# Attention: the halves of the weight sums are added directly behind the next chunk's key product

## The chip, the cores and the metric

The kernel runs on one core of one Trainium2 chip. The metric is the device time of one execution in microseconds (us); lower is better. Three runs of the kernel before took 2790.14, 2790.73 and 2792.69 us, so the time before is the median, 2790.73 us. The profiled execution is a further run with a time of its own, 2798.62 us, and all durations below are from it.

Engine names as the profile writes them: PE is TensorE's matmul, PEld its weight load, DVE is VectorE, ACT is ScalarE, POOL is GpSimd, SP is SyncE. `L708` is line 708 of the kernel before.

## The reference

Four layers over 2048 nodes, a batch of 8 and 128 features, all with the same sparse adjacency matrix (about 1 in 128 entries set). Layers 0 and 1 are masked attention with 8 heads of 16 features, then a projection, a layer norm, a feed-forward net and a second layer norm. Layers 2 and 3 are graph attention (GAT); the change does not touch them.

```python
# layers 0 and 1
Q, K, V = h @ Wq, h @ Wk, h @ Wv            # as (B, N, 8 heads, 16)
scores = einsum('bnhd,bmhd->bhnm', Q, K) / sqrt(16)
scores = where(adj_matrix == 0, -inf, scores)
attn = softmax(scores, axis=-1)
attn_out = einsum('bhnm,bmhd->bnhd', attn, V)
x = layer_norm(h + attn_out @ Wo + bo)
x = layer_norm(x + relu(x @ W1 + b1) @ W2 + b2)
# layers 2 and 3
h = x @ W
e = leaky_relu((h @ a_src)[:, :, None] + (h @ a_dst)[:, None, :])
out = softmax(where(adj == 0, -inf, e)) @ h
x = layer_norm(out + x)
```

The softmax's denominator, the sum of a node's weights per batch entry and head, is what the changed lines compute.

## The kernel before, in words

**Tiling.** The adjacency is turned into lists of neighbours, and nodes are sorted by how many they have. A block is 128 nodes, one per partition; there are 16 blocks in each layer. A block has as many slots as its longest list (`CAPS`, from 29 in the first block down to 10 in the last). A chunk is two slots in layers 0 and 1: each slot is an indirect DMA that gathers one neighbour's keys and values for all 8 batch entries (1 MB per slot) into one of 7 buffers `kv`. So a block is 5 to 15 chunks, and an attention layer is 141 chunks.

**One chunk** (`attention_chunk`, a generator that `go` advances step by step):

1. key product on DVE: keys times queries (`L657`);
2. on DVE the two halves of each head's products are added (`L663`); PE transposes the result eight times into `pair`, which sums the rest (`turn_into`, `L335`); ACT takes the exponent into `ring` (`L679`);
3. PE transposes the weights back (`L683`), ACT copies them to `weights` (`L687`). In a block's last chunk `block_sums` follows: PE adds up the weights of up to seven chunks (`L636`, `L641`) and ACT copies the sum to the tile `partial` (`L646`), whose left and right 64 columns are the two slots of a chunk;
4. on DVE the values are multiplied by the weights (`L695`);
5. and 6. for each slot PE adds eight transposed tiles to the block's accumulator `acc` (`L335`).

**The order around the change.** Every engine works through its own instructions in the order in which the program issues them, and that order is written out by hand in `layers`. Its loop has one iteration per chunk `c`. Within iteration i the order is: step 3 of chunk i-1; step 6 of chunk i-3; step 1 of chunk i; a `slot`; step 2 of chunk i; a `slot`; then `weigh` for chunk i-2, which is its steps 4 and 5; a `slot`. A `slot` advances each side thread (`threads`, `tails`) by one step and issues gathers (`fetch`).

**The sums.** If the chunk that `weigh` takes is the last of its block (call it X), `weigh` first calls `sums`: on DVE the two halves of `partial` are added into `block_sum` (`L708`), ACT takes the logarithm (`L710`), and a thread `scales` is started, which over the next slots takes an exponent on ACT (`L730`, 128x1024), transposes the result on PE (eight times, `L335` into `m`) and copies it on ACT (`L741`, twice). For the last block of a layer `sums` also reduces the smallest and the largest sum on DVE (`L714`, `L715`). So the sum of block X stands in iteration X+2, behind the key products of X+1 and X+2 and both their `L663`, and ahead of X's own `L695`.

**What uses it.** `tail` is started in iteration X+3, and in the fifth slot after that `outputs` multiplies `acc` by `scale` on DVE (`L723`, twice). Then `attention_tail` runs in the slots, in two halves: projection, both norms, the feed-forward net and the next layer's projection. This is work of PE and ACT (`L754` to `L804`, `normed` at `L502` to `L509`, `project` at `L539` to `L549`), issued between the steps of the next block's chunks.

Of the kernel before, what the change touches and what calls it, by code (L numbers as in the profile page):

```python
# [89 lines left out]
def sparse_path(ctx: ExitStack, tc: tile.TileContext, ins: dict, out: bass.AP, flag: bass.AP):  # L90
# [384 lines left out]
    def reciprocal_sums(l, t, w, columns, folded):  # L475

        sums = small.tile([P, columns], F32, tag="sums", name="sums")
        n = CAPS[t] if t > 0 else BASE
        nc.vector.tensor_reduce(
            sums, w[:, :n, :].rearrange("p s c -> p c s"), axis=AX.X, op=ALU.add  # L480
        )
        if t == 0:
            nc.vector.tensor_add(sums, sums, folded)
        nc.vector.tensor_reduce(dmin[:, l, t : t + 1], sums, axis=AX.X, op=ALU.min)
        nc.vector.tensor_reduce(dmax[:, l, t : t + 1], sums, axis=AX.X, op=ALU.max)
        nc.vector.reciprocal(sums, sums)
        return sums
# [217 lines left out]
    def sums(l, t, box):  # L705
        if l < 2:
            both = box["partial"]
            nc.vector.tensor_add(block_sum[:, t, :], both[:, : NB * NH], both[:, NB * NH :])  # L708
            box["r"] = small.tile([P, NB * NH], F32, tag="logs", name="logs", bufs=1)
            nc.scalar.activation(box["r"], block_sum[:, t, :], AF.Ln)  # L710
            threads.append(scales(l, box))
            if t == NT - 1:
                every = block_sum.rearrange("p t c -> p (t c)")
                nc.vector.tensor_reduce(dmin[:, l, :1], every, axis=AX.X, op=ALU.min)  # L714
                nc.vector.tensor_reduce(dmax[:, l, :1], every, axis=AX.X, op=ALU.max)  # L715
            return
        box["r"] = reciprocal_sums(l, t, box["w"], NB, box.get("folded"))
# [7 lines left out]
    def scales(l, box):  # L725

        box["scale"] = scale = work.tile([P, NB, P], F32, tag="oT", name="scale", bufs=1)
        if l < 2:
            r = box["r"].rearrange("p (b h) -> p b h", h=NH)
            nc.scalar.activation(  # L730
                scale.rearrange("p b (j h) -> p b j h", h=NH),
                r[:, :, None, :].to_broadcast([P, NB, HD, NH]), AF.Exp, scale=-1.0,
            )
            yield
        for i in range(0, NB, 4):
            pt = misc()
            for j in range(4):
                r = box["r"][:, i + j : i + j + 1].to_broadcast([P, P])
                turn_into(pt[:, j * P : (j + 1) * P], scale[:, i + j, :] if l < 2 else r, j == 0)
            yield  # L740
            nc.scalar.copy(scale[:, i : i + 4, :].rearrange("p b n -> p (b n)"), pt)  # L741
# [439 lines left out]
    def advance(group):  # L1181
        for g in list(group):
            if next(g, 0) == 0:
                group.remove(g)

    def fetch():

        while now[1] < len(every):
            c = every[now[1]]
            l, t, k, ns = c["l"], c["t"], c["k"], c["ns"]  # L1190

            if now[1] - now[0] > (5 if now[1] >= KVB and every[now[1] - KVB]["l"] > 1 else 4):
                return
            resorted = l > 0 and t < 2 and not c["folded"]
            need = NT - max([b for end, b in EARLY[t] if k + ns <= end] + [0] if resorted else [0])
            if put[l] < need:
                return
            c["buf"] = buffer()[:, : ns * width(l)].rearrange("p (s c) -> p s c", s=ns)
            c["turn"] = turn[0]
            for i in range(ns):  # L1200
                at = t * BASE if resorted else first[t]
                index = (sorted_lists if resorted else lists)[:, at + k + i : at + k + i + 1]
                gather(l, index, c["buf"][:, i], need)
            now[1] += 1

    def hurry():

        c = every[min(now[0], len(every) - 1)]
        return c["l"] == 2 and c["t"] == NT - 1 or c["l"] > 1 and put[c["l"]] < NT

    def slot():
        advance(threads)
        advance(tails)
        fetch()
        beat[0] += 1
        c = every[min(now[0], len(every) - 1)]
        if c["l"] > 0 and put[c["l"]] < NT or beat[0] % 3 == 0 and hurry():
            advance(tails)

    def drain():  # L1220
        while threads or tails:
            advance(threads)
            advance(tails)

    def later(n, make):
        for _ in range(n):
            yield
        yield from make()

    def tail(l, t, box):  # L1230
        for _ in range(4 if l < 2 else 3 if t > NT - 4 else 5):
            yield
        outputs(l, t, box)
        if l < 2:
            tails.append(later(1, lambda: attention_tail(l, t, box, 0)))
            tails.append(later(4, lambda: attention_tail(l, t, box, 4)))
        else:
            tails.append(later(1, lambda: gat_tail(l, t, box)))
        yield
# [9 lines left out]
    def begin(c):  # L1249
        if c["l"] < 2:  # L1250
            threads.append(attention_begin(c["l"], c["t"], c["box"]))

    def chunk(i):
        return every[i] if 0 <= i < len(every) else dict(l=None, k=None, last=False, folded=False)

    def go(c, times=1):

        for _ in range(times if c["l"] is not None else 0):
            next(c["run"], None)

    def weigh(some, added):

        for c2 in some:
            if c2["last"]:
                sums(c2["l"], c2["t"], c2["box"])
            go(c2, 2)
            added.append(c2)

    def layers():
        drain()  # L1270
        begin(every[0])
        drain()
        for _ in weights:
            pass
        threads.append(find_lists(1))
        weighed, added = [], []
        for i in range(len(every) + 2):
            c1, c, n1, n2 = (chunk(i + j) for j in range(-1, 3))
            for c2 in weighed[-1:]:
                go(c2)  # L1280
            while added:
                c2 = added.pop(0)
                go(c2)
                if c2["last"]:
                    threads.append(tail(c2["l"], c2["t"], c2["box"]))
            now[0] = i
            fetch()
            if c["k"] == 0:
                l, t = c["l"], c["t"]
                if l == 0:  # L1290
                    if t + 2 < NT:
                        threads.append(find_lists(t + 2))
                    if t == 0:
                        threads.append(first_states(range(1, NT)))
                        threads.append(later(12, clear_late))
                    if t in (2, 6):
                        threads.append(order_lists(t // 4))
                while l < 2 and "asked" not in c["box"]:
                    slot()
            while i < len(every) and now[1] <= i:  # L1300
                slot()
            if n2["k"] == 0:
                begin(n2)

            if n1["l"] in (2, 3) and n1["folded"]:
                go(n1)
            if c["l"] not in (0, 1) and weighed:
                weigh(weighed, added)  # L1310
                weighed = []
            if c1["l"] in (2, 3) and c1["last"]:
                sums(c1["l"], c1["t"], c1["box"])
                threads.append(scales(c1["l"], c1["box"]))
            go(c)
            slot()
            go(c)
            slot()
            if c["l"] in (0, 1):
                weighed.append(c)  # L1320
            if len(weighed) > 2:
                weigh(weighed[:1], added)
                weighed.pop(0)
            if c1["l"] in (2, 3):
                go(c1, 2)
                if c1["last"]:
                    threads.append(tail(c1["l"], c1["t"], c1["box"]))
            slot()
        verdict()
        drain()  # L1330

    weights = prepare()
    with tc.manual_schedule():
        nc.scalar.add_instruction(
            mybir.InstLoadActFuncSet(name=nc.get_next_instruction_name(), act_func_set_id=LN_EXP)
        )
        start()
        layers()
# [522 lines left out]
```

## Time and profile before

| | |
|---|---|
| median of three runs | 2790.73 us (2790.14 to 2792.69) |
| profiled execution, its time | 2798.62 us |
| its span (first to last instruction) | 2796.7 us |
| start-up, before the first chunk | about 0 to 150 us |
| layer 0 chunks | about 150 to 1041 us |
| layer 1 chunks | about 1041 to 1887 us |
| layers 2 and 3 | about 1887 to 2797 us |
| sums (`L708`) | 32 in all, 16 per attention layer, 0.23 us each |
| key products (`L657`) | 280, 2.2 us each |
| half additions (`L663`) | 282, 1.2 us each |
| value products (`L695`) | 282, 2.2 us each |

The times of the layers are from the timeline; counts and durations are from the page's costliest groups and from the instructions of the tile `block_sum`. The busy share of an engine is over the whole span. A gap of an engine is put down to what ended last before it. A PE row's duration is modelled and pipelined: eight transposes take about 1.04 us as a row, but the next row starts 0.87 us after it.

### The profile page before, as it was taken

To read this page: it belongs to the slowest core of one execution; us is meant where nothing else is said; L and a number is where in the kernel's file an instruction comes from. 1 tells how busy PE (TensorE), PEld (TensorE's weight loads), DVE (VectorE), ACT (ScalarE), POOL (GpSimd) and SP (SyncE) were. 2 spreads that over 40 slices of the span, in tenths; PEclk is the share of its full clock that TensorE was granted. 3 is DMA by queue.
4 is the path that set the end of the run, shared out by engine and by line. 5 is a ranking of instruction groups with operands and counts; after the bars stand their busy time and mean duration, and the time that the engine had idled before them with its cause. 6 is when DMAs were issued, how large, how long until landed. Compare 5 with 4: busy or idle time off the path is not lost.

```text
span 2796.7 us, 48901 instructions
## 1 busy us (share of the span) xinstructions
PE 2345.7 (84%) x17811; PEld 2126.5 (76%) x17811; DVE 2513.7 (90%) x2467; ACT 1381.6 (49%) x5032; POOL 1755.3 (63%) x1346
## 2 busy tenths in 40 slices
PE   5866889898899998798989999997677887878885
PEld 4655788787788887688878888886567776878885
DVE  9698999999899897999999999986889997799995
ACT  3611444454455665154445556566346566355554
POOL 3367788678656454545565566562776776677772
PEclk9978999999999999999999999999789888999997
DMA  9898999999999888789999999984999998999994
GB/s 365 275 373 311 369 349 345 376 338 350 369 337 355 336 320 315 306 320 369 348 390 369 354 374 368 349 328 172 367 412 413 375 367 326 347 411 413 406 402 157
DMA packets 195426, 973.64 MB, mean 348 GB/s; under 512 B 30012, under 2 KB 31804, under 8 KB 123184
## 3 DMA queue, kind: packets, MB, share of 16 engines
q0 software_dynamic: 172080, 885.06, 82.5%
q1 hardware_dynamic: 18346, 60.00, 5.5%
q10 hardware_dynamic: 4752, 25.36, 2.7%
q8 instruction: 144, 2.36, 0.3%
q14 instruction: 104, 0.85, 0.1%
HBM read 917.09 MB, written 87.36 MB: 359 GB/s over the span
## 4 chain that ended last, share of the span: by engine, by line
PE 42%; DVE 24%; DMA 16%; issue 8%; ACT 8%; POOL 1%; ACTq 0%; POOLq 0%; DVEq 0%; SPq 0%
PE acc L335 15%; DMA kv<-table,lists 9%; DVE kv L695 8%; DVE kv L657 8%; PE pair L335 4%; PE m L793 4%; PE m L776 3%; PE m L539 3%; PE m L342 2%; DVE kv L838 2%; PE m L788 2%; PE m L593 2%; PE m L759 2%; PE m L763 2%; DMA table<-rows,perm 2%
## 5 line engine op out<-in xcount | busy, mean ns | idle before, releaser
L321 POOL DMA_INDIRECT kv<-table,lists x938 | 1282.2, 1367 | 678.0 <-PE acc L335 269.8
L335 PE MATMUL acc<-ident,kv 128*128 128x128 f32 x8048 | 1052.9, 285 | 159.6 <-DVE kv L695 87.9
L335 PEld LDWEIGHTS acc<-ident,kv 128*128 128x128 f32 x8048 | 957.6, 148 | 222.4 <-DVE kv L695 111.1
L695 DVE TENSOR_TENSOR kv<-kv,weights 128x2048 f32<-128x2048 f32 (+1 forms) x282 | 625.8, 2219 | 25.9 <-ACT weights L687 25.8
L657 DVE TENSOR_TENSOR kv<-kv,q 128x2048 f32<-128x2048 f32 (+1 forms) x280 | 618.2, 2208 | 32.0 <-DMA kv<-table,lists 26.3
L838 DVE TENSOR_TENSOR kv<-kv,pair 128x3584 f32<-128x3584 f32 (+1 forms) x150 | 530.8, 3538 | 1.0
L335 PE MATMUL pair<-ident,kv 128*128 128x128 f32 (+1 forms) x2256 | 301.3, 277 | 86.1 <-issue 72.8
L663 DVE TENSOR_TENSOR kv<-kv 128x1024 f32<-128x1024 f32 (+1 forms) x282 | 334.8, 1187 | 9.2
L335 PEld LDWEIGHTS pair<-ident,kv 128*128 128x128 f32 (+1 forms) x2256 | 257.0, 141 | 106.4 <-issue 85.1
L321 POOL DMA_INDIRECT kv<-table,sorted_lists x150 | 192.8, 1286 | 139.7 <-PE acc L335 42.9
L679 ACT ACTIVATE ring<-pair 128x128 f32<-128x128 f32 (+1 forms) x282 | 77.8, 276 | 365.0 <-PE pair L335 292.9
L502 ACT ACTIVATE n<-m,eps 128x128 f32<-128x128 f32 x512 | 181.5, 371 | 137.6 <-PE m L793 133.3
L687 ACT COPY weights<-pair 128x128 f32<-128x128 f32 (+1 forms) x282 | 73.3, 260 | 350.9 <-PE pair L683 342.7
L843 ACT ACTIVATE kv<-kv,ws 128x128 f32<-128x128 f32 x544 | 174.5, 398 | 145.0 <-DVE ws L832 136.4
L793 PE MATMUL m<-w_L,hT 128*128 128x128 f32 x1024 | 157.3, 276 | 0.0
L509 ACT ACTIVATE n<-m,rs 128x128 f32<-128x128 f32 x512 | 146.4, 376 | 0.3
L793 PEld LDWEIGHTS m<-w_L,hT 128*128 128x128 f32 x1024 | 136.1, 193 | 0.0
L776 PE MATMUL m<-n1T,w_L 128*128 128x512 f32 x256 | 132.9, 604 | 3.0 <-ACT hT L781 1.8
L723 DVE TENSOR_TENSOR o<-acc,scale 128x512 f32<-128x512 f32 x128 | 83.3, 684 | 52.0 <-ACT scale L741 27.1
L526 POOL DMA_INDIRECT table<-rows,perm x57 | 82.1, 1441 | 70.1 <-ACT own L562 18.7
L342 PE MATMUL m<-ident,n 128*128 128x128 f32 x640 | 114.9, 293 | 11.9 <-ACT n L509 5.6
L342 PEld LDWEIGHTS m<-ident,n 128*128 128x128 f32 x640 | 79.6, 145 | 51.0 <-ACT n L509 23.3
(254 smaller groups left out, 3614.2 us busy)
## 6 DMA issues: line engine op xcount, KB each, us to landing
kept<-xT SPq DMA_DIRECT2D x40, 512.0 KB, 6.7
kv<-in_adj_dram SPq DMA_DIRECT2D x16, 1024.0 KB, 15.6
table<-kv ACTq DMA_DIRECT2D x16, 1024.0 KB, 4.5
xT<-kept SPq DMA_DIRECT2D x32, 512.0 KB, 8.0
kv<-table,lists POOLq DMA_INDIRECT x938, 8.6
kv<-in_x_nodes_dram ACTq DMA_DIRECT2D x16, 512.0 KB, 9.9
kv<-table,sorted_lists POOLq DMA_INDIRECT x150, 6.9
home<-kept SPq DMA_DIRECT2D x4, 512.0 KB, 15.3
```

Source lines behind the costliest of these rows:

```text
L321: this = nc.gpsimd.indirect_dma_start(out=dst, out_offset=None, in_=tables[l][:, :] if need == NT else views[l][0], in_offset=bass.Indirec ...
L335: nc.tensor.matmul(dst, src, ident, start=start, stop=True, is_transpose=True, skip_group_check=True)
L342: nc.tensor.transpose(pt[:, j * P : (j + 1) * P], src[:, j, :], ident)
L502: nc.scalar.activation(dst[:, i, :], z[:, i, :], AF.Square, bias=eps, scale=D**-0.5, accum_out=ss[:, i : i + 1],)
L509: nc.scalar.mul(dst[:, i, :], z[:, i, :], rs[:, i : i + 1])
L657: nc.vector.tensor_mul(kk, kk, q[:, None].to_broadcast([P, ns, NB, D]))
L663: nc.vector.tensor_add(hk.rearrange("p j (c h) -> p c j h", h=NH), kj[:, :, :NH, :], kj[:, :, NH:, :])
L695: nc.vector.tensor_mul(vv, vv, w.rearrange("p (s b h) -> p (s b) h", b=NB, h=NH)[:, :, None, :] .to_broadcast([P, ns * NB, HD, NH]),)
L776: nc.tensor.matmul(ph, wt["1"][:, f * P : (f + 1) * P], n1T.rearrange("p b c -> p (b c)"), start=True, stop=True,)
L793: nc.tensor.matmul(y[:, j, :], hT[:, f, j, :], wt["2"][:, f, :], start=False, stop=f == 1, skip_group_check=True,)
L838: nc.vector.tensor_mul(hv[:, :, :nv, :], hv[:, :, :nv, :], wc[:, :, :nv, None].to_broadcast([P, ns, nv, D]))
L843: nc.scalar.mul(hv[:, i, b, :], hv[:, i, b, :], ws[:, i, b - nv : b - nv + 1])
```

## The change

For layers 0 and 1 the call of `sums` moves out of `weigh` and into the loop of `layers`, directly behind step 1 of the chunk that follows the block's last one. It then stands in iteration X+1, behind the key product of chunk X+1 and ahead of its `L663`. The thread `scales` is started there too, so logarithm, exponent, transposes and copies of the scale all move up by about five slots. For the very last block of layer 1 the next chunk is one of layer 2; there the order before was sum, value product `L695` of X, first step of the GAT chunk, and it becomes `L695` of X, first step of the GAT chunk, sum. Layers 2 and 3 are called as before.

```diff
     def weigh(some, added):
 
         for c2 in some:
-            if c2["last"]:
+            if c2["last"] and c2["l"] > 1:
                 sums(c2["l"], c2["t"], c2["box"])
             go(c2, 2)
             added.append(c2)
...
             go(c)
+            if c1["l"] in (0, 1) and c1["last"]:
+                sums(c1["l"], c1["t"], c1["box"])
             slot()
             go(c)
             slot()
```

Here `c` is the chunk of the iteration and `c1` the one before it.

## Prediction

> **What bounds the kernel now.** I read the page's busy times first, then the same by stretches, then the waits of the tile `partial` and of DVE, and last the timeline around one sum. X is a block's last chunk, as above.
>
> The page's first part, for the whole span:
>
> ```profile
> PE 2345.7 (84%) x17811; PEld 2126.5 (76%) x17811; DVE 2513.7 (90%) x2467; ACT 1381.6 (49%) x5032; POOL 1755.3 (63%) x1346
> ```
>
> The busy times of two stretches inside the attention layers (length, then us and instructions of PE, PEld, DVE, ACT, POOL, then granted clock, DMA share, GB/s):
>
> ```profile
> 250.00:1041.00 791.00, 712.76 (x5445) 638.06 (x5444) 739.26 (x589) 396.13 (x1359) 547.46 (x337) 0.97 0.92 352
> 1106.00:1887.00 781.00, 707.71 (x5566) 638.28 (x5565) 744.05 (x443) 383.37 (x1448) 455.71 (x278) 0.97 0.92 353
> ```
>
> DVE is busy 93 and 95% of them. It never has more than short gaps, so whatever makes it wait longer lengthens the layer, unless an existing gap takes it up. PE is at 90 and 91%, and it waits for DVE, not only the other way round. From the view of who waited for whom (total, times, longest):
>
> ```profile
> PE acc L335 <- DVE kv L695: 87.9, 76, 3.5
> ...
> DVE o L723 <- ACT scale L741: 27.1, 19, 9.9
> ...
> DVE kv L657 <- DMA kv<-table,lists: 26.3, 15, 6.5
> ...
> DVE kv L695 <- ACT weights L687: 25.8, 15, 5.2
> ```
>
> The second line is what the change can save. What it can cost is in the tile `partial`: already now, two chunks behind X, the sum sometimes waits for it.
>
> ```profile
> L646 ACT COPY partial<-m x57: 266/266/270, 196.7 to 1887.1; 128x128 f32<-128x128 f32 x57
> ...
> who waited for it (us, times):
>   DVE block_sum L708: 17.3, 12
> ```
>
> DVE's timeline around the sum of layer 0's tenth block (block 9):
>
> ```profile
> 776.71 2.28 DVE L657 TENSOR_TENSOR kv<-kv,q 128x2048 f32<-128x2048 f32 x1
> 779.03 1.23 DVE L663 TENSOR_TENSOR kv<-kv 128x1024 f32<-128x1024 f32 x1
> 780.36 2.29 DVE L695 TENSOR_TENSOR kv<-kv,weights 128x2048 f32<-128x2048 f32 x1
> 782.57 2.29 DVE L657 TENSOR_TENSOR kv<-kv,q 128x2048 f32<-128x2048 f32 x1
> 784.89 1.23 DVE L663 TENSOR_TENSOR kv<-kv 128x1024 f32<-128x1024 f32 x1
> 788.46 0.23 DVE L708 TENSOR_TENSOR block_sum<-partial 128x64 f32<-128x64 f32 x1 [2.34 <-ACT partial L646]
> ```
>
> and PE's and ACT's, where `partial` is made:
>
> ```profile
> 786.94 0.27 PE L683 MATMUL pair<-ident,ring 64*128 64x64 f32 x1
> 787.06 0.22 PE L636 MATMUL m<-ident,ring 64*128 64x64 f32 x1
> 787.21 0.49 PE L641 MATMUL m<-partial,ident 128*128 128x128 f32 x2
> 787.53 1.04 PE L335 MATMUL acc<-ident,kv 128*128 128x128 f32 x8
> ```
>
> ```profile
> 788.16 0.27 ACT L646 COPY partial<-m 128x128 f32<-128x128 f32 x1
> ```
>
> The first two DVE rows are the key product and half addition of X+1, the fourth and fifth those of X+2. The key product of X+1 ends at 778.99; `partial` is finished at 788.43. PE runs 9 us behind DVE, because here it works off the attention tail of the block before. DVE uses that lead for a half addition, a value product and all of X+2.
>
> **The change, part by part.**
>
> *The moved sum.* In the changed program's order the sum stands directly behind the key product of X+1 in 31 of the 32 blocks; it issues no DMA, and the sequences of POOL and SP stay as they are. It needs `partial`, and nothing that `partial` needs comes later on DVE, so DVE stops from the end of that key product to the end of the copy: in block 9 788.43 - 778.99 = 9.4 us. Behind it on DVE queue the half addition of X+1 (for which PE's transposes and ACT's exponent wait) and the value product of X-1 (for which PE's `acc` waits). The same subtraction on the timeline of every block, in us:
>
> - layer 0, blocks 0 to 14: 0 (`partial` 3.5 earlier), 1.9, 4.3, 4.4, 1.2, 5.9, 7.4, 5.8, 4.0, 9.4, 8.3, 7.5, 7.6, 7.7, 2.9: 78.4;
> - layer 1, blocks 0 to 14: 1.8, 6.8, 2.9, 3.9, 4.3, 4.7, 7.0, 7.0, 9.0, 9.7, 8.3, 5.8, 7.6, 7.7, 2.8: 89.4.
>
> Together 167.8 us in 30 blocks. Can it be less than a full charge? Only if DVE was ahead for nothing. The time from the end of a half addition to ACT's exponent of it is 4 to 10 us just behind a block's end and falls to 1.2 to 2.5 us within the next block, before its own end nears (the layers' last blocks apart, which come below). So between any two sums there is a place where DVE sets the pace, and a lead taken from it is time.
>
> *Gaps that go.* A stopped DVE has no later gap of the same origin. The sums' own waits: 17.3, less 3.3 (last block of layer 1) and 0.7 (last of layer 0), 13.3 us. The outputs' waits for the scale: it is started five slots sooner, so 27.1, less the 10.2 at layer 0's end, 16.9 us. The value products' waits for `weights`, PE's lag again: 25.8, less 9.3 around layer 1's start and 1.7 in the middle of a block, 14.8 us. Sum -45.1 us. Block 9 nets 9.4 - 2.3 - 1.2 = 5.9 us. Of the key products' DMA waits those close behind a sum may be taken up too: between 0 and 11 us (all after the first block's), I take -5, the ones within 10 us behind a sum (1.3, 1.9, 0.5) and a neighbouring wait of 1.0.
>
> *Logarithm, exponent, scale.* ACT's logarithm waits for the sum, and behind it queue the exponent of 1.06 us, X+1's `ring` and what the old tail has left. In layer 1's last block, where nothing was between, the exponent ended 1.6 us behind the sum's start (1887.36 to 1888.97). PE's first scale transposes need it; they stand behind X+1's eight transposes, which end 0.2 + 1.2 + 0.9 = 2.3 us behind the sum's start. So they don't wait, and I cost the move at nothing. Were the cover gone, 1.6 - 1.2 = 0.4 us a block, 12 us in all, would be the bound above; the bound below is the 16.9 already taken.
>
> *Layer 0's last block.* Its stop is 7.6 us, and the two reductions (1.2 us each) now also come ahead of X+1's half addition. But from 1030 to 1070 PE has hardly a gap and DVE has 12.7 us of them just behind (2.4 for `weights`, 10.2 for the scale). So PE sets the pace there and loses only what it waits for X+1's half addition: `partial` at 1041.2 + 0.2 + 2.4 + 1.2 = 1045.0, 2.2 us past the old start of its transposes, 1042.86; with ACT's tail held behind the exponent I take +3, bounds -5 (7.6 - 12.7) and +10 (7.6 + 2.4).
>
> *Layer 1's last block.* The sum goes later, behind X's value product and the first GAT step. That product then waits for `weights`, about 1886.8, not for the sum at 1887.4, and the reductions (2.4 us) follow it: a gain of 3.0 us for PE's `acc`, a loss of 2.5 us for the scale, used 20 us later. Zero, bounds -3 and +3.
>
> *Sum.* 167.8 - 45.1 - 5 + 3 + 0 = +120.7 us on the profiled execution's 2798.6 (span 2796.7 and 1.9 around it), 2919.3. That execution is 7.9 us, 0.28%, above the median of the runs, so 2790.7 + 120.7 = 2911 us.
>
> *Two rules of the Trainium skill.* The row is the outputs' wait for the scale, 27.1 us. "Perfetto Trace Analysis", section Optimization Strategy, says to look for the gaps of the busiest engine and make what they wait for start sooner; taken alone that gives 2764 us, and it speaks for the change. It leaves out that the earlier start has an input of its own, late by 5.6 us on the average of 30 blocks.
>
> The second row is the granted clock, 0.97 in both stretches. "TensorE: Matmul & The Clock Gate", section HAM oscillation, says that PE gaps over some 3.4 us cost the clock; it speaks against the change, since PE will idle more. The longest wait of PE's `acc` for DVE is 3.5 us at that 0.97. With the clock of the GAT layers (0.90), PE's 1420 us in the two stretches would grow by 110, an upper estimate by that rule of 3020 us; I take none of it, since PE's new stops are single ones of about 2 us.
>
> **The rivals.**
>
> *PE is the bound, DVE's lead is slack.* Then each stop costs only what PE idles: 0.2 + 1.2 us of sum and half addition, less the 0.9 us of `acc` transposes queued behind `partial`, and about as much again before the value product of X-1 arrives, at most 2 us: 30 x 2 - 16.9 = +43, 2834 us. For it: PE's 90%, and the lag of 8 to 10 us at block ends. Against it: PE's 87.9 us of waits for value products, and the lag that falls back in each block.
>
> *Faster: the scale's wait goes and no new one comes.* This happens if PE reaches `partial` before X+1's key product ends, as in layer 0's first block (3.5 us early). All stops zero: -45.1 - 5 + 3, 2744 us. It decides when the mean stop is under 45.1/30 = 1.5 us; only two of the 30 blocks are under that. For it: the tail's pace may change with the order. Against it: 28 blocks.
>
> *Partly taken up.* If all those DMA waits go and the stops shrink by a quarter because the next tail starts from a caught-up PE: 126 - 45 - 11 + 3 = +73, 2863 us. For it: the lag behind a sum is gone by the time of the next tail. Against it: that lag reaches its floor before the next tail in the kernel before, too.
>
> That the change doesn't do what it says is excluded by the program's order.
>
> **How the numbers follow.** 0.2% (5.6 us) is about what a measurement of this kernel can tell from no change. Forecast 0.78; partly taken up 0.09; PE the bound 0.09; faster 0.03; and 0.01 for no change. Around the forecast: above, no scale gap gone, the exponent uncovered, and layer 0's end at its bound, of which I grant 30 together: 2940. Below, the partly taken-up case: 2863. What is left out, PE the bound, faster and the same, and a tail above, is under 0.2. Slower 0.96, same 0.01, faster 0.03.
>
> **What would show it.** Right: the sum waits for `partial` in about 30 blocks, some 165 us in all, in place of 17.3; the outputs wait for the scale only at layer 0's end, if at all; DVE's busy time stays 2514 us and the two stretches lengthen by about 55 to 65 us each; the layers from 1887 on keep their 909 us. Wrong: a wait of the sums well under 100 us, or layers that lengthen by much less than it, or a granted clock off 0.97.

## The result and the profile after

The changed kernel takes 2905.7 us (median of 6 runs, 2900.89 to 2911.41) against 2790.43 us for the kernel before on the same chip (6 runs): 1.0412 times as long, 95% interval 1.0396 to 1.0428. That is 115.3 us slower; 120.7 had been predicted. The profiled execution took 2910.61 us, its span is 2908.8, against 2796.7: 112.1 us longer.

The first part of the page, busy time, share of the span and instructions of each engine, after:

```profile
PE 2382.1 (82%) x17811; PEld 2150.2 (74%) x17811; DVE 2508.0 (86%) x2467; ACT 1384.3 (48%) x5032; POOL 1757.9 (60%) x1346
```

The counts of these instructions are the same to the last one, and DVE's busy time even fell by 5.7 us. Only its share fell, from 90 to 86%: the added time is time in which DVE stands. Where it stands is told by the view of who waited for whom (us in total, times, longest):

```profile
DVE block_sum L708 <- ACT partial L646: 184.7, 30, 9.7
...
PE acc L335 <- DVE kv L695: 119.2, 100, 2.3
...
DVE o L723 <- PE acc L335: 25.2, 4, 17.1
...
DVE kv L657 <- DMA kv<-table,lists: 13.5, 6, 5.9
...
DVE kv L695 <- ACT weights L687: 11.6, 5, 5.2
```

The first row was 17.3 us in 12 waits; now all but two of the 32 sums wait, 6.2 us on the average. The row in which outputs waited for the scale (27.1 us) is gone altogether. The second row shows who pays behind DVE: PE's accumulations waited 87.9 us for value products before and 119.2 now. This is DVE's timeline around the sum of the tenth block (start, duration, operation; idle time before it and what ended it in brackets):

```profile
798.24 2.29 DVE L657 TENSOR_TENSOR kv<-kv,q 128x2048 f32<-128x2048 f32 x1
808.90 0.23 DVE L708 TENSOR_TENSOR block_sum<-partial 128x64 f32<-128x64 f32 x1 [8.37 <-ACT partial L646]
809.04 1.22 DVE L663 TENSOR_TENSOR kv<-kv 128x1024 f32<-128x1024 f32 x1
810.17 2.29 DVE L695 TENSOR_TENSOR kv<-kv,weights 128x2048 f32<-128x2048 f32 x1
```

Between the key product of X+1 and its half addition DVE does nothing for 8.4 us. Before, the half addition, a value product and all of X+2 were done in that time. PE and ACT meanwhile are still at the attention tail of the block before, and `partial` comes behind it. PE reaches its last product (`L641`) only here:

```profile
806.42 1.04 PE L335 MATMUL acc<-ident,kv 128*128 128x128 f32 x8
807.65 0.49 PE L641 MATMUL m<-partial,ident 128*128 128x128 f32 x2
```

On ACT the copy to `partial`, the logarithm and the exponent then follow closely:

```profile
808.50 0.19 ACT L687 COPY weights<-pair 128x64 f32<-128x64 f32 x1
808.60 0.27 ACT L646 COPY partial<-m 128x128 f32<-128x128 f32 x1
809.16 0.26 ACT L710 ACTIVATE logs<-block_sum 128x64 f32<-128x64 f32 x1 [0.29 <-DVE block_sum L708]
809.44 1.06 ACT L730 ACTIVATE scale<-logs 128x1024 f32<-128x1024 f32 x1
```

The busy times by stretch, after (length; us and instructions of PE, PEld, DVE, ACT, POOL; granted clock, DMA share, GB/s). The first two are the stretches shown of before, the last two begin where the layers are under way and end at about their new ends:

```profile
250.00:1041.00 791.00, 687.54 (x5134) 613.18 (x5133) 698.64 (x565) 373.17 (x1279) 534.60 (x325) 0.95 0.90 336
1106.00:1887.00 781.00, 670.36 (x5063) 598.10 (x5062) 677.13 (x402) 350.06 (x1299) 392.24 (x248) 0.95 0.87 328
250.00:1099.00 849.00, 739.96 (x5516) 656.88 (x5515) 744.67 (x594) 408.87 (x1396) 555.68 (x340) 0.96 0.89 332
1164.00:1999.00 835.00, 720.32 (x5465) 644.06 (x5464) 728.03 (x436) 382.40 (x1439) 430.79 (x268) 0.95 0.86 321
```

In the same 791 us DVE is idle for 92 us, where it was idle for 52; in the 781 us of layer 1 for 104, where it was 37. Both layers together are 116 us longer: the reduction at the end of layer 1 starts at 2003.6 us, not 1887.6. The view of the tile `dmin` shows it (minimum, median and maximum duration in ns, then the first and the last start), of before:

```profile
L714 DVE TENSOR_REDUCE dmin<-block_sum x2: 1219/1220/1221, 1041.5 to 1887.6; 128x1 f32<-128x1024 f32 x2
```

and of after:

```profile
L714 DVE TENSOR_REDUCE dmin<-block_sum x2: 1220/1220/1220, 1082.6 to 2003.6; 128x1 f32<-128x1024 f32 x2
```

From there to the end of the span it is 905.2 us (909.1 before), so the GAT layers took no part. I use the second start below as the end of the attention stage.

**The account.** DVE's idle time before and after, by what ended it, in us:

| DVE waits in the attention stage | before | after | difference | predicted |
|---|---|---|---|---|
| sums for `partial` | 17.3 | 184.7 | +167.4 | +158.1 |
| outputs for the scale | 27.1 | 0 | -27.1 | -27.1 |
| value products for `weights` | 25.8 | 11.6 | -14.2 | -17.2 |
| key products for a gather | 26.3 | 13.5 | -12.8 | -5 |
| outputs for PE's `acc` | 0 | 5.5 | +5.5 | 0 |
| key products for `q` | 4.6 | 11.4 | +6.8 | 0 |
| list ordering at the layer's start | 4.5 | 0 | -4.5 | 0 |

The rest of the `acc` row shown above, 16.8 us before and 19.7 after, lies in the GAT layers. These rows and DVE's busy time in the stage (1735.2 us before, 1732.6 after, -2.6) come to +118.4 us; rows of about 1 us and less and gaps too short for the view make -2.4, and that is the 116.0 us of the stage. The predicted column comes to 108.8 because it takes the two layer ends row by row: for layer 0's end the sum's stop of 7.6 less its old wait of 0.7, less 10.2 for the scale and 2.4 for `weights`, -5.7, where the prediction charged +3, and for layer 1's end the sum's old wait of 3.3, where it charged nothing. With those two it is the prediction's 120.7 again.

### The profile page after: what moved, and what is told of

Same layout as the page of the kernel before. It is cut to its first block, busy times and chain, and to the rows that moved or that the text cites. A ratio compares the mean times of both kernels' runs of the same rounds, so it can differ in the third digit from the quotient of the medians.

```text
span 2908.8 us, 48904 instructions
## 1 busy us (share of the span) xinstructions
PE 2382.1 (82%) x17811; PEld 2150.2 (74%) x17811; DVE 2508.0 (86%) x2467; ACT 1384.3 (48%) x5032; POOL 1757.9 (60%) x1346
## 4 chain that ended last, share of the span: by engine, by line
PE 44%; DVE 27%; DMA 12%; issue 9%; ACT 6%; POOL 1%; ACTq 0%; POOLq 0%; DVEq 0%; SPq 0%
PE acc L335 15%; DVE kv L695 9%; DVE kv L657 8%; DMA kv<-table,lists 7%; PE pair L335 4%; PE m L793 4%; PE m L776 4%; DVE kv L838 3%; PE m L539 3%; PE m L342 3%; PE m L593 2%; PE m L788 2%; DVE kv L663 2%; DVE o L723 2%; PE m L759 2%
## 5 line engine op out<-in xcount | busy, mean ns | idle before, releaser
L321 POOL DMA_INDIRECT kv<-table,lists x938 | 1259.5, 1343 | 780.1 <-PE acc L335 364.8
L335 PE MATMUL acc<-ident,kv 128*128 128x128 f32 x8048 | 1074.9, 288 | 188.6 <-DVE kv L695 119.2
L335 PEld LDWEIGHTS acc<-ident,kv 128*128 128x128 f32 x8048 | 973.5, 149 | 257.8 <-DVE kv L695 149.3
L657 DVE TENSOR_TENSOR kv<-kv,q 128x2048 f32<-128x2048 f32 (+1 forms) x280 | 618.0, 2207 | 25.3 <-DMA kv<-table,lists 13.5
L695 DVE TENSOR_TENSOR kv<-kv,weights 128x2048 f32<-128x2048 f32 (+1 forms) x282 | 625.8, 2220 | 11.6 <-ACT weights L687 11.6
L335 PE MATMUL pair<-ident,kv 128*128 128x128 f32 (+1 forms) x2256 | 304.5, 279 | 134.3 <-issue 101.4
L663 DVE TENSOR_TENSOR kv<-kv 128x1024 f32<-128x1024 f32 (+1 forms) x282 | 334.5, 1186 | 8.2
L708 DVE TENSOR_TENSOR block_sum<-partial 128x64 f32<-128x64 f32 x32 | 7.2, 225 | 184.7 <-ACT partial L646 184.7
L526 POOL DMA_INDIRECT table<-rows,perm x57 | 91.0, 1597 | 63.3 <-ACT own L562 15.0
```

The source lines that it names most:

```text
L321: this = nc.gpsimd.indirect_dma_start(out=dst, out_offset=None, in_=tables[l][:, :] if need == NT else views[l][0], in_offset=bass.Indirec ...
L335: nc.tensor.matmul(dst, src, ident, start=start, stop=True, is_transpose=True, skip_group_check=True)
L657: nc.vector.tensor_mul(kk, kk, q[:, None].to_broadcast([P, ns, NB, D]))
L663: nc.vector.tensor_add(hk.rearrange("p j (c h) -> p c j h", h=NH), kj[:, :, :NH, :], kj[:, :, NH:, :])
L695: nc.vector.tensor_mul(vv, vv, w.rearrange("p (s b h) -> p (s b) h", b=NB, h=NH)[:, :, None, :] .to_broadcast([P, ns * NB, HD, NH]),)
```

## The experiments

**My theory**: DVE's lead over PE at a block's end is worth time, since DVE sets the pace a little later; the sum stands behind PE's and ACT's backlog, and waiting for it there takes the lead away. It is the place of this one 0.23 us addition that costs. **Rivals**: the early logarithm, exponent and scale cost it in ACT's and PE's queues; or PE is the bound and the stops are largely slack. Later I also asked whether there is a place or an engine for the addition that keeps the early scale and loses nothing.

The experiments were made on three chips. On the second and third the kernel before takes 2917.16 and 2903.49 us; in the traces from there the GAT layers take some 1000 to 1040 us, while the attention stage is about as long as on the first (for the changed kernel it ends at 1999.3 us on the third and 2003.6 on the first). So every ratio is against the kernel before on the same chip, and the end of the attention stage is compared across chips.

### Only the addition early

```diff
 def sums(l, t, box):              # called where the change put it
     nc.vector.tensor_add(block_sum[:, t, :], both[:, : NB * NH], both[:, NB * NH :])
-    box["r"] = ...; nc.scalar.activation(box["r"], block_sum[:, t, :], AF.Ln)
-    threads.append(scales(l, box))
 ...
+    if (l, t) == (1, NT - 1):                # layer 1's last block as in the change
+        logs(l, t, box)
 ...
 def weigh(some, added):
+    elif c2["last"] and (c2["l"], c2["t"]) != (1, NT - 1):
+        logs(c2["l"], c2["t"], c2["box"])    # Ln and scales, at their old place
```

> Only the sum on VectorE moves up, to where the changed kernel has it; logarithm, exponent and scale start where they started before (the last block of layer 1 as in the changed kernel). Theory (VectorE is stopped by the wait for `partial`, and its lead is time): the sums wait about 185 us as in the changed kernel and the time stays near it, 2895 to 2915 us. Rival (the logarithm, the exponent and the scale's transposes, put ahead of other work on ScalarE and TensorE, are what costs): the time falls back to 2790 to 2810 us.

Measured: 2906.62 us, ratio 1.042 (1.0393 to 1.0446), the same as the whole change. Its waits:

```profile
DVE block_sum L708 <- ACT partial L646: 184.1, 30, 9.7
...
DVE kv L695 <- ACT weights L687: 11.3, 5, 5.2
...
DVE o L727 <- ACT scale L745: 8.2, 4, 7.4
```

The addition alone carries the whole loss, and the early logarithm and scale carry nothing of it. There is a second finding. The scale is started at its old place here, and yet of the outputs' 27.1 us of waits for it only 8.2 are left, 7.4 of them in one wait at layer 0's end. So within the layers the stop removed these waits, by letting PE and ACT catch up, and not the earlier start.

### The addition at two later places

Behind X-1's value product in iteration X+1 (3.4 us of DVE work later than the change has it; logarithm and scale follow it):

```diff
             go(c)
-            if c1["l"] in (0, 1) and c1["last"]:
-                sums(c1["l"], c1["t"], c1["box"])
 ...
                 weigh(weighed[:1], added)
                 weighed.pop(0)
+            if c1["l"] in (0, 1) and c1["last"]:    # layer 1's last block as in the change
+                sums(c1["l"], c1["t"], c1["box"])
```

> The sum one half addition and one value product later than in the changed kernel (3.4 us of VectorE work), still in the iteration behind the block's last chunk. Theory: each wait of the changed kernel shrinks by 3.4 us, from 185 to 87 us in all; the outputs' wait for the scale stays gone, the other gaps that went come back in part: 2790 + 87 - 17 - 35 = 2825 us (2805 to 2840). Rival (a fixed price for each early sum, whatever the length of the wait): 2870 us or more.

Behind the key product of X+2 (5.65 us later, and still 1.2 us of DVE work ahead of its place in the kernel before):

```diff
             go(c)
-            if c1["l"] in (0, 1) and c1["last"]:
-                sums(c1["l"], c1["t"], c1["box"])
+            c0 = chunk(i - 2)
+            if c0["l"] in (0, 1) and c0["last"]:    # layer 1's last block as in the change
+                sums(c0["l"], c0["t"], c0["box"])
```

> The sum behind the key product of the second chunk after the block (5.65 us of VectorE work later than in the changed kernel, one half addition earlier than before). Theory: the waits shrink to about 37 us, only 20 more than before, and the outputs' 27 us of waits for the scale are mostly gone: 2783 us (2770 to 2800). Rival (fixed price): 2870 us or more.

Measured: 2819.47 us, ratio 1.0111 (1.0077 to 1.0144), and 2798.26 us, ratio 1.003 (1.0018 to 1.0042). The waits of the first:

```profile
DVE block_sum L708 <- ACT partial L646: 74.0, 22, 5.8
...
DVE kv L657 <- DMA kv<-table,lists: 20.9, 12, 6.5
...
DVE kv L695 <- ACT weights L687: 18.6, 14, 5.2
```

and of the second:

```profile
DVE block_sum L708 <- ACT partial L646: 33.5, 14, 3.6
DVE kv L657 <- DMA kv<-table,lists: 31.6, 19, 5.8
...
DVE kv L695 <- ACT weights L687: 21.7, 17, 5.2
DVE o L723 <- PE acc L335: 20.2, 7, 14.6
...
DVE o L723 <- ACT weights L687: 9.3, 1, 9.3
```

With the kernel before and after this is a scale of four places:

| place of the sum, DVE work behind X+1's key product | waits of the sums | attention stage ends | time against before |
|---|---|---|---|
| 0 (the change) | 184.7 us | 2003.6 us | +115 us |
| 3.4 us | 74.0 | 1919.5 | +29 |
| 5.65 us | 33.5 | 1895.0 | +8 |
| 7 us (before) | 17.3 | 1887.6 | 0 |

The time follows the waits: each 3.4 us of lead that DVE keeps is worth nearly that much in each of 30 blocks at the first step (86 us of 102), and less where many blocks no longer wait. For the first place I had expected 2805 to 2840 us, and that held. For the second I had expected a gain from the scale's waits, and it is slightly slower: within the layers the outputs wait only 1.0 us for the scale, but 3.1 for PE's `acc` (the rest of that row lies in the GAT layers), and at layer 0's end they still wait 9.3. That wait is put down to `weights`, which they don't read; PE's transposes into `acc` end at the same moment. The key products wait 31.6 us for their gathers where it was 26.3. The waits for the scale were a symptom of PE's lag, not its cause.

### The addition taken from DVE altogether

PE already adds up the weights for `partial`. Multiplied by two identities, one above the other, instead of transposed, it adds the two halves too, and DVE needs no sum. Once with logarithm and scale at the changed place, and once, as a control, at the old one:

```diff
+    ident2 = const.tile([P, NB * NH], F32, name="ident2")
+    nc.vector.tensor_add(ident2, ident[:, : NB * NH], ident[:, NB * NH :])
 ...
-                ps[:, :m], e, ident[:m, :m], ..., is_transpose=True,
+                ps, e, ident2[:m, :], ...,
 ...
-        nc.scalar.copy(box["partial"], ps)
+        nc.scalar.copy(block_sum[:, t, :], ps)     # where it is the block's last
 ...
-            nc.vector.tensor_add(block_sum[:, t, :], both[:, : NB * NH], both[:, NB * NH :])
```

> TensorE adds the halves itself (the transposes of `block_sums` multiply by two identities stacked on each other instead of one), so VectorE has no sum and no wait; logarithm and scale start where the changed kernel has them. Theory: without the wait on VectorE the early scale is a gain, about the 17 to 27 us of the outputs' waits, while the sums' 17 us mostly turn into waits for `weights`: 2770 us (2760 to 2785). Rival (the early logarithm, exponent and scale cost): slower than before, 2800 us or more.

> The control for TensorE adding the halves: the same addition on TensorE, logarithm and scale at the kernel before's place. The addition there cost 280 more TensorE instructions (18091 against 17811). If that work is why the version with the early scale came out at 2814 us, and the early scale itself is a gain of some 20 us, this one is slower still: 2815 to 2845 us. If the early logarithm, exponent and scale are what cost, this one is back near the kernel before: 2785 to 2800 us.

Measured: 2813.74 us, ratio 1.0095 (1.0071 to 1.012), with the early scale; on another chip 2941.26 us, ratio 1.0061 (1.0041 to 1.0081), with the late one. Without any stop of DVE for `partial` the loss is under 1%, which confirms where the 4.1% lay (only the reduction at layer 0's end still waits, 9.5 us). But the gain that I had expected, 2770 us, did not come, and the control shows one reason: PE's part costs time by itself. The multiplications of the weights stand in the view of their line as `x560`, where before they were `x280`:

```profile
L638 PE MATMUL m<-ident,ring x560: 222/275/422, 194.7 to 1903.8; 128*128 128x64 f32 x174, 64*128 64x64 f32 x13
```

```profile
L636 PE MATMUL m<-ident,ring x280: 222/273/418, 195.2 to 1886.7; 128*128 128x128 f32 x132, 64*128 64x64 f32 x8
```

The first is the experiment, the second the kernel before. A 32-bit product that is no transpose is issued as two instructions here, each as long as the one transpose, though it has 64 columns where the transpose has 128. Between the two places of the scale the ratios differ by some 0.3%, to the disadvantage of the early one, but the two intervals overlap, by the medians both are 24 us above the kernel before, and the attention stage ends sooner with the early one (1906.0 against 1912.9 us). In the late version the outputs wait 27.8 us for the scale in the stage, in the early one not at all; but there the value products wait 65.4 us for `weights`, where in the late one all their waits come to 51.5. So most of what the early scale saves at the outputs comes back elsewhere; whether it gains or costs a little stays open.

### Added work on DVE, with the wait and without it

If DVE's lead is time, then work that is added where DVE waits anyway is free. If PE is the bound, added work is nearly free in the kernel before too. A reduction over 2048 elements, whose result nobody uses, is put behind the key product of X+1 in 31 blocks, in the kernel before and in the changed one (ahead of the sum):

```diff
             go(c)
+            if c1["l"] in (0, 1) and c1["last"] and (c1["l"], c1["t"]) != (1, NT - 1):
+                extra = small.tile([P, NT], F32, tag="extra", name="extra", bufs=1)
+                nc.vector.tensor_reduce(
+                    extra, ident[:, None, :].to_broadcast([P, NT, P]), axis=AX.X, op=ALU.add
+                )
```

> The kernel before, with one VectorE reduction of 128x2048 (some 2.3 us by the 128x1024 one's 1.2) put behind the key product of the chunk that follows a block's last one, in 31 blocks; nobody uses its result. Theory (VectorE's lead at that place is time): about 31 x 2.3 = 71 us less what existing gaps of the block take up, at most 2.3 us in each of 17 blocks, about 31 us: 2830 us (2815 to 2845). Rival (TensorE sets the pace there, VectorE's lead is slack): 2790 to 2800 us.

> The changed kernel with the same reduction, between the key product and the moved sum. Theory: it runs inside the wait for `partial`, which shrinks by its 2.3 us wherever it was longer; only the first block and parts of two others remain: 2905 + 5 = 2910 us (2900 to 2918), and the sums' waits fall from 185 to about 117 us. Rival (each early VectorE instruction has its price whatever it waits for): 2960 to 2980 us.

In both it takes 31 times 2.278 us, 70.6 us. In the kernel before: 2934.11 us, ratio 1.0058 (1.0024 to 1.0091), about 17 us, and the attention stage ends 21 us later. In the changed kernel: 3024.55 us, ratio 1.0335 (1.0295 to 1.0374), with the attention stage ending at 2002.9 us where the changed kernel's ended at 2003.6. The changed kernel hadn't run on that chip, so both were run once more together on a third one:

> The changed kernel itself once more, so that the one with an added VectorE reduction is compared with it on one chip: ratio to before 1.036 to 1.043.

> The changed kernel with a 128x2048 VectorE reduction in 31 blocks between key product and sum (69 us of VectorE work), on the same chip as the changed kernel. Theory: the work runs inside the wait for `partial`, at most 5 us slower than the changed kernel, and the sums' waits fall by about 67 us. Rival (VectorE's work counts whatever it waits for): 60 to 70 us slower than the changed kernel.

Measured: 3016.04 us, ratio 1.0387 (1.0337 to 1.0437), for the change alone, and 3016.45 us, ratio 1.0381 (1.0341 to 1.0421), with the added work. 70.6 us of DVE work cost 0.4 us, within the spread of the runs, and in the traces the attention stage ends no later (1995.4 us, against 1999.3 for the change alone). In the view of the tile `partial`, what ended the idle time ahead of the tile's instructions, for the change alone:

```profile
  ACT partial L646: 125.6, 22
  ACT weights L687: 27.9, 4
  ACT rs L493: 24.7, 3
```

and with the added work:

```profile
  ACT partial L646: 77.1, 20
  ACT weights L687: 37.3, 8
```

(A wait for several semaphores is put down to the one that came last by the profile; here ACT's copies of `weights` and `rs` stand directly ahead of `partial`, so all these are the sum's waits.) They fall from 178.2 us (182.6 with one that the view puts down to no one) to 114.4: the added work lies in the wait and takes 64 to 68 us of it away, nearly its own length. So the stop is a wait that DVE's work can fill without delay to anyone, and it is ended by PE and ACT.

The other half of the test is less clean. In the kernel before I had expected the added 70.6 us to cost at least 25, and the rival at most 10; 17 to 21 lie between. DVE's other waits took up more than I had reckoned with: the sums' own 17.3 us fell to 4.6, the value products' 25.8 for `weights` to 13.0, the key products' 26.3 for gathers to 10.2, the outputs' 27.1 for the scale to 21.5, together 47.2 us. In the first stretch DVE's idle time halved, from 51.7 to 25.9 us:

```profile
250.00:1041.00 791.00, 710.31 (x5410) 634.80 (x5411) 765.12 (x602) 392.90 (x1351) 548.68 (x336) 0.97 0.92 349
```

So it isn't true of the kernel before that whatever delays DVE lengthens the layer one for one: 2.3 us a block cost 0.6 us. A stop of 6 us a block exceeds the slack.

### The addition on GpSimd

```diff
-            nc.vector.tensor_add(block_sum[:, t, :], both[:, : NB * NH], both[:, NB * NH :])
+            nc.gpsimd.tensor_add(block_sum[:, t, :], both[:, : NB * NH], both[:, NB * NH :])
```

> The changed kernel with the sum on GpSimd instead of VectorE, at the same place of the program; it waits for `partial` there, ahead of gathers. Theory (only VectorE's stop costs): VectorE has no stop, the outputs have no wait for the scale, and GpSimd, whose gathers wait for TensorE to release buffers at that point anyway, hides the wait: 2775 us (2760 to 2790). If the gathers behind the sum become late, the key products wait for DMA instead and it is 2800 us or more. Rival (the early logarithm, exponent and scale cost something): 2795 to 2815 us without such DMA waits.

Measured: 3051.15 us, ratio 1.0419 (1.0376 to 1.0462). DVE has no stop for `partial` any more, and the loss is at least as large as before: the attention stage ends at 2024.6 us, 21 us later than the changed kernel's. The expectation fell. The waits:

```profile
ACT logs L710 <- POOL block_sum L708: 168.9, 32, 17.8
...
DVE kv L695 <- ACT weights L687: 167.2, 40, 10.4
...
DVE dmin L714 <- POOL block_sum L708: 32.1, 2, 16.5
```

ACT works in order too. Its logarithm now waits for GpSimd, and behind it the exponents and the copies to `weights` are held, for which DVE's value products wait 167 us. One such sum on GpSimd's timeline:

```profile
866.80 1.54 POOL L321 DMA_INDIRECT kv<-table,lists  x1 [0.56 <-PE acc L335]
868.36 1.49 POOL L708 TENSOR_TENSOR block_sum<-partial 128x64 f32<-128x64 f32 x1
```

and on ACT's:

```profile
866.11 0.27 ACT L646 COPY partial<-m 128x128 f32<-128x128 f32 x1
869.88 0.26 ACT L710 ACTIVATE logs<-block_sum 128x64 f32<-128x64 f32 x1 [3.50 <-POOL block_sum L708]
```

`partial` is finished at 866.38; the sum starts 2 us later, behind a gather that itself had waited for a buffer, and takes 1.49 us (median 0.55, where DVE needs 0.23). Would GpSimd do if ACT's queue were left alone? The same with logarithm and scale at their old place, as in the first experiment:

> The sum on GpSimd at the changed kernel's place, but logarithm and scale at the kernel before's. With the early logarithm, that sum made ScalarE wait 169 us for GpSimd, and everything behind it in ScalarE's queue. If that queue is what cost 4.2%, it is gone here: 2780 to 2800 us on the chip of the first runs (ratio to before 0.995 to 1.004). If GpSimd's wait and the gathers behind it cost too, the ratio stays above 1.01 and the key products wait for DMA.

Measured: 2939.61 us, ratio 1.0109 (1.0071 to 1.0147). Three quarters of the loss are gone with ACT's queue freed. Still 7 logarithms wait 36.3 us for the sum, and the reductions at the two layer ends 28.8 us in two waits:

```profile
ACT logs L720 <- POOL block_sum L708: 36.3, 7, 15.6
...
DVE dmin L711 <- POOL block_sum L708: 28.8, 2, 15.5
```

The key products wait 30.5 us for their gathers, hardly more than the 26.3 before. The two rows could make up the rest; I didn't separate them.

### The scale sooner, the addition not

DVE's order as in the kernel before, the sum behind the half addition of X+2, but issued one slot sooner, so that only logarithm, exponent and scale gain a slot:

```diff
     def weigh(some, added):
-            if c2["last"]:
+            if c2["last"] and (c2["l"] > 1 or (c2["l"], c2["t"]) == (1, NT - 1)):
                 sums(c2["l"], c2["t"], c2["box"])
 ...
             slot()
             go(c)
+            c0 = chunk(i - 2)
+            if c0["l"] in (0, 1) and c0["last"] and (c0["l"], c0["t"]) != (1, NT - 1):
+                sums(c0["l"], c0["t"], c0["box"])
             slot()
```

> VectorE's order exactly as in the kernel before; only the logarithm and the scale's thread start one slot sooner (the sum is called right behind step 2 of the second chunk after the block, not one slot later). Theory (the outputs' waits for the scale are idle time of the bounding engine, and nothing new waits): 5 to 15 us faster than before, 2775 to 2787 us, with the outputs' 27 us of waits for the scale roughly halved. Rival (these gaps only hold time that the next wait takes anyway, as the late scale next to the early sum showed no difference): within 0.2% of before.

Measured: 2900.6 us over 12 runs, ratio 0.9984 (0.9961 to 1.0007). It isn't told apart from the kernel before. The outputs still wait for the scale:

```profile
DVE o L723 <- ACT scale L741: 23.1, 12, 8.5
```

23.1 us against 27.1 (the latter on the first chip). I found no version that is measurably faster than the kernel before.

## Why the prediction was right, and where it was not

**The stops of DVE**, +167.8 us in 30 blocks by subtraction on the old timeline. Measured 176.2 in the same 30 (83.5 in layer 0, 92.7 in layer 1; 78.4 and 89.4 predicted). Of the 30 blocks 20 lie within 1 us of their subtraction, among them the first block's 0, and none is off by more than 2; the tenth's is 8.4 for 9.4. The term was 8.4 us too small, 5%. That a stop is time, the step on which the forecast differed from the rivals, is shown by the first experiment (the addition alone), by the scale of four places and by the pair with added work.

**"The outputs' waits for the scale: it is started five slots sooner", -16.9.** The size held: none are left within the layers. The reason was wrong. With the scale started late they vanish as well, since the stop lets PE catch up; and where the scale starts sooner without a stop no gain could be measured. The Trainium skill's "Perfetto Trace Analysis", section Optimization Strategy, says to find the gaps of the engine and make what they wait for start sooner. The estimate of 2764 us, worked out from this row alone, fails in both ways here: the sooner start has a price, and the gap wasn't where the time was lost.

**The value products' waits for `weights`**, -14.8: measured -14.2 over the attention stage, or -17.4 without a new one of 3.1 us at layer 1's end; with layer 0's end -17.2 had been forecast.

**The key products' waits for gathers**, -5 with bounds 0 and -11. Measured -12.8, and the waits of the list ordering fell by another 4.5: the term was mis-sized, and even its bound was short. Waits farther than 10 us behind a sum were taken up too: of the 11 us behind the first block none is left. Their waits for `q`, +6.8, stood nowhere in the prediction. The gathers' error and that of the stops have opposite signs, and it is partly their luck that the sum came within 5.4 us of the measured difference.

**Layer 0's last block**, +3. Its stop is 8.5 us (7.6 predicted), the wait for the scale there (10.2) is gone, and 5.5 us of new waits of the outputs for PE's `acc` came, which is PE setting the pace there, as argued. The price of that end can be read off DVE's two timelines: the key product just ahead of the stop starts 40.3 us later than before (1071.55 and 1031.28), one well into layer 1 44.3 (1162.56 and 1118.29). That is +4.0, for +3.

**Logarithm and exponent at nothing.** Confirmed by the first experiment on the changed order: 2906.62 against 2905.7 us. Behind each sum the time from a half addition to its exponent is 1.2 to 1.8 us now. Before, it was 1.4 to 10.1 us; the prediction's "4 to 10" holds for 24 of 31 blocks, and the others are the ones with short stops. **Layer 1's last block at nothing**: its sum waits for nothing in after, and the value product now ahead of it waits 3.1 us for `weights`, as argued. DVE's lag behind the old timeline is 113.5 us at the layer's last key product and 113.4 at the outputs of that block.

**The rivals.** "PE is the bound" gave 2834 us and fell by the time; its idea that a lead is partly slack is nevertheless true for small delays (2.3 us a block cost a quarter of itself). "Partly taken up" rested on shrinking stops and they grew. "Faster" needed a mean stop under 1.5 us; it is 5.9.

**The signs named beforehand.** About 30 waits of 165 us: 30 of 184.7. DVE busy 2514: 2508. The GAT layers 909 us: 905. The two layers each 55 to 65 us longer: uneven, 48 in layer 0 (the first reduction starts 41.1 us later, though it stands 6.9 us of DVE work sooner in the order) and 65.5 in layer 1 (the second stands 2.5 us later in the order).

**The clock.** A granted clock off 0.97 was named as a sign of error: it is 0.95 to 0.96 in the attention stretches. PE's waits grew from 87.9 to 119.2 us for value products and from 72.8 to 101.4 ahead of the transposes into `pair` (longest 5.9 us, 5.3 before). The Trainium skill's "TensorE: Matmul & The Clock Gate", section HAM oscillation, has it that PE gaps over some 3.4 us cost the clock. In the attention stage from 250 us on there are two such gaps before (3.9 and 5.3 us) and one after (5.9), the clock in these stretches fell by 0.01 to 0.02, and a loss like the estimate of 3020 us isn't borne out. The clock is not what cost, either: in the first experiment it is 0.97 from 250 us to the end of the stage, as in the kernel before (0.95 in the changed one), and the loss is the same. PE's busy time in the stage rose from 1645.5 to 1686.3 us, and to 1679.5 in that experiment; a row's end is modelled, and I didn't look into how much of this is real.

## What to carry to other kernels

Before an operation is moved up in an in-order queue, subtract on the old timeline: the moment its input is finished less the moment its engine will now reach it. What comes out is a stop for everything behind it. Putting the operation on another engine helped here only as far as no third engine's queue waited for it: on GpSimd it cost 4.2% with ACT's logarithm directly behind it and 1.1% without. A wait that one wants to remove should first be asked what it is a symptom of: here the outputs waited for a scale because PE was behind, and starting the scale sooner gained nothing that could be measured.

## What the runs showed that was not expected

- A 32-bit product that isn't a transpose is issued to PE as two instructions of the same length as the one transpose (560 against 280 for the same weights; 0.275 us with 64 columns and 0.273 with 128 in the median).
- A 128x64 addition of 0.23 us on DVE takes 0.33 to 1.5 us on GpSimd (median 0.55 in one experiment and 1.01 in the other), and it starts behind whatever gathers stand ahead of it.
- 70.6 us of work on the busiest engine can cost 0.4 us (in a wait) or 17 (in the kernel before, whose short gaps took up 47 us).
- The same kernel's GAT layers took 905 us at a granted clock of 0.90 on one chip and 1007 us at 0.85 on another, at 353 and 317 GB/s; the attention stage hardly differed (2003.6 and 1999.3 us). The cause wasn't looked into.
